# Statistics, routing and turned logits behind the attention step, another front, keys turned by transfers, and eight attention steps per block in a layer of linear attention plus a mixture of experts

## The chip, the cores and the metric

The kernel runs on one core of one Trainium2 chip. The metric is the device time of one execution in microseconds (us), median of the runs shown. The engines are named as in the profile: PE (matrix products and transposes through the array), PEld (its weight loads, beside PE), DVE (vector), ACT (activation), POOL (indirect transfers and accumulating stores, small vector work), SP (issues most of the transfers).

## What is computed

One layer over x of shape (8, 1024, 256), float32. With xn = (x - mean)/sqrt(var + 1e-5) per row:

```python
q, k = elu(xn @ Wq.T) + 1, elu(xn @ Wk.T) + 1;  v = xn @ Wv.T      # 16 heads of 16
out   = q . cumsum(k v) / clip(q . cumsum(k), 1e-6)                # causal linear attention
attn  = out @ Wo.T
logits = x_n @ Wr + br            # 8 experts; the two best, softmax over their two logits
ffn   = sum over the two of  c_e * (silu(xn @ W1[e]) * (xn @ W3[e])) @ W2[e]     # inner width 512
result = x + attn + ffn
```

Here x_n is xn too: both branches take the normalised rows.

## The kernel before, in words

The 8192 rows are 16 **blocks** of 512 rows (t, four chunks c of 128). Two kinds of work share the engines.

**The experts.** Rows are sorted by expert into **tiles** of 128 rows (j); 132 tiles are run here. A tile step (`tile_step`, with `ffn_step` inside) gathers its rows by an indirect transfer on POOL (xg, and a table entry with mean, deviation and weight), normalises them on ACT (L1231), turns them so that features lie on partitions (xgT: tiles below 27 on PE, later ones by a transfer of 16-bit halves, L1241, L1250, L1259), makes gate and up (gu_ps, L1310, 16 products of 128x128x128, 32 records in the profile), silu on ACT (L1318), the product on DVE (hT, L1321), one tile later the product with W2 (y_ps, L1329), its scaling on DVE (y, L1336) and an accumulating scatter on POOL (L1340). W1 and W3 of a tile are loaded by SP two tiles ahead into five buffers.

**The attention.** `attention()` is a generator of steps, block by block (`block_steps`, `project`, `scores`, `carry`, `weigh`, `attend`), and every tile step takes about one of them (`attend_upto`) ahead of its own products. Nine steps make a block: queries (zq L819); keys (zkk L835, then elu on ACT and DVE into kn); the keys turned on PE (tp L882: 8 transposes, kT copied from PSUM by ACT L885) with running sums on DVE (ksum: a scan L887, its last column L891, the product with the queries L892); values (zkv L835, copied into va by ACT L852) and denominators (den L904, then L910 and L911 on DVE and eight transfers of rden by SP); the scores of chunk 0 (s_ps L936, masked by DVE into s_sb L943); and four steps, one for each chunk (o_ps L955, L973, L983, then oT L990 and kv L993 on DVE). PE's order is the program's (`manual_schedule`), DVE's, ACT's and POOL's behind the front is set by a planner from priorities and expected readiness; each engine runs its own list in order.

**The front.** Four blocks are loaded, normalised, turned and routed first (first_moments, normalise, turn, logits, `route`), and `first_batch` makes the list of the first 25 tiles from them: one-hot rows made by ACT (mid_at), POOL (late_at, L650) and DVE (at_first), summed on PE (sum_ps L704), copied by ACT (sums L711), summed again (first_ps L713), made into row numbers (num_i L617). The first gather waits for these. The front is one order written by hand on all engines.

**Tiles 0 to 11** also bring in the other 12 blocks: statistics two blocks at a time (`moments`, L312 to L330), `normalise` (ACT, four a block), `turn` (tp L358, xnT copied by ACT), `logits` (lg_ps L376, copied to lgT by ACT L1424, turned on PE L1437) and, every four blocks, `route` (some fourteen DVE operations L424 to L457, then cnt_ps L463 and L469 on PE). From tile 12 on `second_batch` makes the list of the other tiles in 32 pieces (at_place L591, held L604 and parts L609 on DVE, parts L611 on ACT, held_ps L749 on PE), spread over tiles 13 to 21.

PSUM is eight banks: four of tag mm (gu, z, s_ps), two of tag y (y_ps, lg, den, a_ps, cnt, sum), two of tag t (tp, xg_t, o_ps).

Of the kernel before, what the change touches and what calls it, by code (L numbers as in the profile page):

```python
# [54 lines left out]
P = 128  # L55
# [9 lines left out]
def tile_attention_moe(  # L65
# [38 lines left out]
    WARMING = 14  # L104
# [155 lines left out]
    nc.gpsimd.memset(va, 0.0)  # L260
# [3 lines left out]
    nc.gpsimd.memset(own_of, 0.0)  # L264
# [3 lines left out]
    nc.gpsimd.tensor_scalar(upto_neg, before, -1.0, None, ALU.add)  # L268
    base_row = iota("base_row", E, ROWS, 0, 0)

    for o in range(KC):
        nc.gpsimd.tensor_copy(own_of[:, o, o * HALF : (o + 1) * HALF], own)
# [11 lines left out]
    def first_moments(t):  # L284
# [3 lines left out]
        for c in range(NCH + 1):  # L288
            if c < NCH:
                nc.vector.bn_stats(st[:, c, :], xbs[t][:, c, :])  # L290
            if c > 0:
                nc.vector.bn_aggr(mv[:, c - 1, :], st[:, c - 1, :])
            if t == FB and c == 1:
                yield
# [7 lines left out]
    def moments(t, n):  # L302


# [4 lines left out]
        st = small("st", 6)  # L309
        mv = small("mv", 2)  # L310
        for c in range(n * NCH):
            nc.vector.bn_stats(st[:, c, :], xbs[t + c // NCH][:, c % NCH, :])  # L312
            nc.vector.bn_aggr(mv[:, c, :], st[:, c, :])
# [15 lines left out]
        yield  # L329
        nc.vector.scalar_tensor_tensor(less, mv[:, :, 0], -1.0, rstd, ALU.mult, ALU.mult)  # L330
        yield

    def normalise(t):
        xb = xbs.pop(t)
        less, rstd = (tab[:, t * NCH : (t + 1) * NCH, w] for w in (1, 2))
        for c in range(NCH):
# [5 lines left out]
            else:  # L342
                nc.scalar.activation(
                    xb[:, c, :], xb[:, c, :], AF.Identity, bias=less[:, c : c + 1],
                    scale=rstd[:, c : c + 1],
                )
        scaled[t] = xb
# [56 lines left out]
    nc.gpsimd.memset(new, 1.0)  # L404
    nc.gpsimd.memset(new[:, :, 0:1], 0.0)
# [4 lines left out]
    def route(a, b):  # L410
# [39 lines left out]
        yield  # L450
# [9 lines left out]
        )  # L460
        cnt_ps = ps_y.tile([P, E * n + E], F32, tag="y", name="cnt_ps")
# [9 lines left out]
        )  # L471
        yield
# [14 lines left out]
        den2 = work("den2", n)  # L487
        nc.vector.tensor_scalar(den2, diff, 1.0, None, ALU.add)
        wt = tab[:, tiles, 0]
        nc.vector.reciprocal(wt, den2)  # L490
        second = slice(NT + a * NCH, NT + b * NCH)
        nc.vector.tensor_tensor(tab[:, second, 0], diff, wt, ALU.mult)
        if a > 0:
            nc.vector.tensor_copy(tab[:, second, 1:3], tab[:, tiles, 1:3])
        yield
# [101 lines left out]
    def one_hot(in_row, place, rows, j, a, n):  # L597
# [11 lines left out]
        nc.vector.tensor_scalar(parts[:, :, 0, :], held, row128[:, 0:1], None, ALU.mult)  # L609
# [22 lines left out]
    def first_batch():  # L632
# [7 lines left out]
        late = FT - 2 * PART  # L640
# [3 lines left out]
        less_place = f_one.tile([P, late], F32, name="less_place")  # L644
        nc.scalar.mul(less_place, place[:, 1, 0:late], -1.0)
        place_f = f_one.tile([P, 2 * PART], F32, name="place_f")
        nc.gpsimd.tensor_copy(place_f, place[:, 1, late:FT])
        late_at = [masked.tile([P, PART, P], F32, tag="s_sb", name="late_at") for _ in range(2)]
        for i in range(2 * PART):
            nc.gpsimd.tensor_scalar(  # L650
                late_at[i // PART][:, i % PART, :], cols, place_f[:, i : i + 1],
                number1[:, FT + late + i : FT + late + i + 1], ALU.is_equal, ALU.mult,
            )
        upto = add_up(sizes(False), "upto1")
# [13 lines left out]
        mid_at = [masked.tile([P, PART, P], F32, tag="s_sb", name="mid_at") for _ in range(2)]  # L668
        for i in range(late):
            nc.scalar.activation(  # L670
                mid_at[i // PART][:, i % PART, :], cols, AF.Square,
                bias=less_place[:, i : i + 1],
            )
            nc.scalar.activation(
                mid_at[i // PART][:, i % PART, :], mid_at[i // PART][:, i % PART, :], AF.Relu,
                bias=number1[:, FT + i : FT + i + 1], scale=from_last[:, i : i + 1],
            )

# [9 lines left out]
        yield  # L688
        sum_ps = ps_y.tile([P, P], F32, tag="y", name="sum_ps")
        groups = [(late_at, 2), (None, 0), (mid_at, 0), (mid_at, 1), (None, 1), (late_at, 3)]  # L690
        groups += [(None, 2), (None, 3)]
        for n, (made, g) in enumerate(groups):
            if made is None:
                at = at_places(
                    place, 0, g * PART,
                    e_two.tile([P, PART, P], F32, tag="at_first", name="at_first"),
                )
            else:
                at = made[g % 2]
            if n == 1:  # L700
                yield
            for i in range(PART):
                c = N1 * ((0 if made is None else FT) + g * PART + i)
# [79 lines left out]
    def elu1(dst, z):  # L783

        neg = two.tile([P, TB], F32, tag="neg", name="neg")
# [40 lines left out]
    def mask_q(t, o):  # L826
        qT, qm = blocks[t][0:2]
        for a in range(2):
            nc.scalar.mul(qm[:, o, a, :], qT[:, o, :], par[:, a : a + 1])

    def project_kv(t, c, a):
        z = ps_mm.tile([P, 2, H], F32, tag="mm", name="zkv"[:2] + "kv"[a])
# [8 lines left out]
    def project_k(t, c):  # L841
# [3 lines left out]
            kn[:, c : c + 2, :].rearrange("p c h -> p (c h)"), z.rearrange("p c h -> p (c h)")  # L845
# [11 lines left out]

    def project(t):


        if t > 0:
            begin(t)
            for o in range(KC):
# [3 lines left out]
                yield  # L867
            for c in range(0, NCH, 2):
                for _ in project_k(t, c):
                    pass  # L870
                yield
        else:
            for _ in range(4):
                yield
        qT, qm, kT, kn, va, rden = blocks[t]
        upto_t = two.tile([P, KC], F32, tag="upto_t", name="upto_t")
        fresh = t % BLK_PER_SEQ == 0
        qks = []
        for o in range(KC):
            tp = ps_t.tile([P, TB], F32, tag="t", name="tp")  # L880
            for c in range(NCH):
                nc.tensor.transpose(  # L882
                    tp[:, bass.ts(c, P)], kn[:, c, bass.ts(o, P)], ident
                )
            nc.scalar.copy(kT[:, o, :], tp)  # L885
            ksum = two.tile([P, TB], F32, tag="ksum", name="ksum")
            nc.vector.tensor_tensor_scan(  # L887
                ksum, ones[:, 0:1].to_broadcast([P, TB]), kT[:, o, :],
                0.0 if fresh else sums[0][:, o : o + 1], ALU.mult, ALU.add,
            )  # L890
            nc.vector.tensor_copy(upto_t[:, o : o + 1], ksum[:, TB - 1 : TB])  # L891
            nc.vector.tensor_tensor(ksum, qT[:, o, :], ksum, ALU.mult)  # L892
            qks.append(ksum)
            yield
        for c in range(0, NCH, 2):
            if t > 0:
                for _ in project_v(t, c):
                    pass
            yield

        den = ps_y.tile([P, P], F32, tag="y", name="den")
# [19 lines left out]
        yield  # L921
# [110 lines left out]
    def block_steps(t):  # L1032


        for i, _ in enumerate(project(t)):
            if i in (1, 3, 5, 8):
                yield
# [21 lines left out]
    STEPS = 9  # L1059
    LAST = NBLK * STEPS + 1  # L1060

    TOGETHER = (0, 4, 8)
# [22 lines left out]
    with tc.manual_schedule(engines={EN.DVE, EN.Activation, EN.PE, EN.Pool}):  # L1085
# [9 lines left out]
        next(parts[0])  # L1095
        for t in range(FB):
            next(parts[t + 1])
            next(parts[t])
            normalise(t)
            if t == 2:  # L1100
                nc.scalar.copy(lgT4[:, 0, :], lg_ps.pop(0))
            turn(t)
# [6 lines left out]
            else:  # L1109
                lg_ps[t - 1] = logits(t - 1)  # L1110
        next(parts[FB])
# [425 lines left out]
```

## Time and profile before

| what | us |
|---|---|
| median of 3 runs (lowest, highest) | 1265.2 (1262.7, 1265.59) |
| the profiled execution: its time | 1257.66 |
| its span, first to last instruction | 1255.5 |
| busy: PE, DVE, ACT, POOL | 1205.5, 675.3, 554.5, 527.9 |
| mean granted clock of PE | 0.987 |
| tile 0's gate and up begin | 51.1 |
| tile 2's gate and up begin | 69.1 |
| PE waits over 0.15 us each from 69.1 to 300, sum | 17.4 |

A row of the groups or of the timeline reads: line of the kernel, engine, operation, out<-in, partitions x elements, count; then busy us and mean ns of one; in brackets the engine's idle time ahead of it and what ended that. In the chain of waits each piece follows the one that released it, with start and length in us, and the PE pieces there are start to start, so that they add up to the time that PE's stream needs. Windows give the busy us of each engine in a stretch, and at the end the granted clock, the share of the 16 DMA engines and GB/s.

### The profile page before, as it was taken

Reading aid. Unit: us, or ns where it says so; the run is one execution under the profiler, and the core shown is the slowest. Engines: PE = TensorE matmul, PEld = TensorE weight load, DVE = VectorE, ACT = ScalarE, POOL = GpSimd, SP = SyncE. Lnnn points to the kernel's source line nnn. Section 1 sums busy time; section 2 is a strip of 40 time slices with the busy share of each in tenths; the row PEclk is TensorE's granted clock in tenths of the full one; section 3 lists DMA queues with packets and bytes.
Section 4 is the critical chain, followed back from the end, with each engine's and each line's share of the span. In section 5 each row is a group of like instructions: output and inputs, shape, how many; then the busy total and the mean of one; then the engine's idle time right before and its main releaser. Section 6 shows DMA issues by size and latency. Waiting matters only on the chain.

```text
span 1255.5 us, 29756 instructions
## 1 busy us (share of the span) xinstructions
PE 1205.5 (96%) x11460; PEld 1059.7 (84%) x11460; DVE 675.3 (54%) x1541; ACT 554.5 (44%) x1064; POOL 527.9 (42%) x460
## 2 busy tenths in 40 slices
PE   7788898999999999999999999999999999999994
PEld 5677787888888889888888889989888889898884
DVE  7776669975344544545453545445453545445451
ACT  5665454471624335262625335262626243352610
POOL 4733234325443544444434544444443354444322
PEclk8899999999999999999999999999999999999997
DMA  9788565747987887969888787979897987879672
GB/s 339 274 276 266 150 209 116 237 115 229 245 196 182 193 198 167 244 151 227 177 200 182 187 202 167 223 169 223 185 200 171 189 193 178 205 165 247 145 178 33
DMA packets 203934, 245.84 MB, mean 196 GB/s; under 512 B 72946, under 2 KB 127858, under 8 KB 203506
## 3 DMA queue, kind: packets, MB, share of 16 engines
q1 hardware_dynamic: 161010, 191.79, 52.9%
q0 software_dynamic: 38032, 43.22, 24.6%
q10 hardware_dynamic: 4752, 8.91, 2.0%
q8 instruction: 94, 1.54, 0.5%
q14 instruction: 46, 0.38, 0.1%
HBM read 187.91 MB, written 44.29 MB: 185 GB/s over the span
## 4 chain that ended last, share of the span: by engine, by line
PE 87%; DVE 7%; DMA 2%; ACT 2%; issue 1%; SPq 0%; POOL 0%; POOLq 0%; ACTq 0%; DVEq 0%
PE gu_ps L1310 36%; PE y_ps L1329 17%; PE s_ps L936 5%; PE o_ps L973 5%; PE a_ps L1015 5%; PE zq L819 4%; PE zkk L835 4%; PE zkv L835 4%; PE o_ps L955 2%; DMA xb<-in_x_dram 1%; PE tp L882 1%; PE held_ps L749 1%; PE tp L358 1%; PE den L904 1%; DVE st L312 1%
## 5 line engine op out<-in xcount | busy, mean ns | idle before, releaser
L1310 PE MATMUL gu_ps<-xgT,w 128*128 128x128 f32 x4224 | 504.6, 277 | 6.4 <-issue 2.9
L1310 PEld LDWEIGHTS gu_ps<-xgT,w 128*128 128x128 f32 x4224 | 487.3, 192 | 21.1 <-issue 12.7
L1340 POOL DMA_INDIRECT out_dram<-y,dst_i x107 | 175.4, 1639 | 320.2 <-DVE y L1336 96.8
L1329 PE MATMUL y_ps<-w_sb,hT 128*128 x1056 | 250.9, 380 | 2.1 <-DVE tab L327 1.1
L1218 POOL DMA_INDIRECT xg<-in_x_dram,src_i x132 | 129.0, 977 | 229.1 <-DVE half L1241 114.4
L1329 PEld LDWEIGHTS y_ps<-w_sb,hT 128*128 128x128 f32 x1056 | 190.5, 190 | 24.8 <-issue 1.6
L1318 ACT ACTIVATE hT<-gu_ps 128x512 f32<-128x512 f32 x132 | 78.8, 597 | 286.9 <-PE gu_ps L1310 237.4
L943 DVE TENSOR_TENSOR s_sb<-s_ps,causal 128x512 f32<-128x512 f32 x256 | 159.0, 681 | 70.5 <-PE s_ps L936 68.1
L1321 DVE TENSOR_TENSOR hT<-gu_ps,hT 128x512 f32<-128x512 f32 x132 | 90.3, 684 | 63.0 <-PE gu_ps L1310 28.2
L1223 POOL DMA_INDIRECT entry<-tab_d,of_i x107 | 107.2, 1002 | 39.5 <-issue 31.4
L1336 DVE TENSOR_SCALAR y<-y_ps,entry 128x256 f32<-128x256 f32 x132 | 63.7, 482 | 109.9 <-PE y_ps L1329 109.9
L1241 DVE COPY half<-xg 128x512 uint16<-128x512 uint16 x105 | 47.9, 457 | 130.7 <-ACT xg L1231 130.7
L1020 ACT COPY at<-a_ps 128x256 f32<-128x256 f32 x64 | 23.8, 373 | 173.0 <-PE a_ps L1015 123.0
L1259 ACT COPY xgT<-halfT 128x512 uint16<-128x512 uint16 x105 | 79.7, 759 | 5.1 <-DMA halfT<-half 5.1
L1231 ACT ACTIVATE xg<-xg,entry 128x256 f32<-128x256 f32 x132 | 78.4, 595 | 2.1 <-DMA entry<-tab_d,num_i 2.1
L936 PE MATMUL s_ps<-qm,kT 32*128 32x256 f32 x1024 | 75.3, 400 | 0.1
L1015 PE MATMUL a_ps<-wo_sb,oT 128*128 128x256 f32 x256 | 67.9, 388 | 2.9 <-DVE y L1336 2.0
L973 PE MATMUL o_ps<-s_sb,va 128*32 128x128 f32 x2048 | 69.2, 276 | 0.0
L973 PEld LDWEIGHTS o_ps<-s_sb,va 128*32 128x32 f32 x2048 | 52.0, 109 | 17.8 <-issue 15.9
L1340 POOL DMA_INDIRECT acc_d<-y,src_i x25 | 44.2, 1766 | 52.6 <-DVE y L1336 23.3
L835 PE MATMUL zkv<-wkv_sb,xnT 128*128 128x256 f32 x256 | 59.9, 388 | 0.0
L835 PE MATMUL zkk<-wkv_sb,xnT 128*128 128x256 f32 x256 | 59.4, 386 | 0.0
(228 smaller groups left out, 1339.1 us busy)
## 6 DMA issues: line engine op xcount, KB each, us to landing
w<-in_w_dram SPq DMA_DIRECT2D x264, 512.0 KB
rden<-over SPq DMA_DIRECT2D x128, 64.0 KB
xnT<-xnT_d SPq DMA_DIRECT2D x15, 512.0 KB
out_dram<-at POOLq DMA_DIRECT2D x13, 512.0 KB
out_dram<-in_x_dram SPq DMA_DIRECT2D x12, 512.0 KB
xnT_d<-xnT ACTq DMA_DIRECT2D x11, 512.0 KB
xb<-in_x_dram SPq DMA_DIRECT2D x9, 512.0 KB
w_sb<-in_w_dram SPq DMA_DIRECT2D x4, 1024.0 KB
```

What stands on the lines that cost most here:

```text
L835: nc.tensor.matmul(z[:, i, :], lhsT=xnTs[t][:, k, bass.ts(c + i, P)], rhs=wkv_sb[:, k, a, :], start=(k == 0), stop=(k == KC - 1),)
L936: nc.tensor.matmul(s_ps[r][:, hh].rearrange("p a l -> p (a l)"), lhsT=kT[rows, hh, span], rhs=qm[rows, hh, :, span], start=True, stop=True,)
L943: last_masked[0] = nc.vector.tensor_tensor(sm, s_ps[r].rearrange("p k a l -> p (k a) l"), causal_b, ALU.mult)
L973: nc.tensor.matmul(o_ps[32 * r : 32 * r + 32, hh, :], lhsT=va[:, c, 4 * hh + r, a, :], rhs=s_sb[r][:, 2 * hh + a, :], start=(first and a = ...
L1015: nc.tensor.matmul(a_ps, lhsT=oT[:, hh, :], rhs=wo_sb[:, hh, :], start=(hh == 0), stop=(hh == 1),)
L1218: rows = nc.gpsimd.indirect_dma_start(out=xg[j], out_offset=None, in_=x_rows[:, :], in_offset=bass.IndirectOffsetOnAxis(ap=src_i[:, i : i ...
L1223: nc.gpsimd.indirect_dma_start(out=entry[j], out_offset=None, in_=table[:, :], in_offset=bass.IndirectOffsetOnAxis(ap=num_i[:, i : i + 1], ...
L1259: nc.scalar.copy(xgT[j].bitcast(U16).rearrange("p k (l b) -> p b k l", b=2), halves.pop(j).rearrange("p (b k) l -> p b k l", b=2),)
L1310: done = nc.tensor.matmul(ps[:, i, :], lhsT=w13[:, k, bass.ts(i, P)], rhs=xgT[j][:, k, :], start=(k == 0), stop=(k == KC - 1),)
L1321: nc.vector.tensor_tensor(hT, gu[1], hT, ALU.mult)
L1329: done = nc.tensor.matmul(y_ps, lhsT=hT[:, i, :], rhs=w2_sb[:, bass.ds(e * (IC * H) + i * H, H)], start=(i == 0), stop=(i == IC - 1),)
L1340: nc.gpsimd.indirect_dma_start(out=rows[:, :], out_offset=bass.IndirectOffsetOnAxis(ap=dst_i[:, i : i + 1], axis=0), in_=ys.pop(j), in_off ...
```

## The change

Five edits, all in the one function:

1. **Front.** Constants not needed at once (new, upto_neg, own_of, va) go behind the five square-root calls on POOL; block 0 is normalised ahead of block 1's statistics; one-hot rows: ACT 8 (BY_ACT), POOL 7 (up to BY_POOL = 15; it made 8), DVE 1; queries' and keys' elu and the query masks (mask_q) go behind the list, the masks behind tile 0's turn; 18 idle products at the start instead of 14, four in the routing, 14 of 128 columns ahead of tile 0 instead of 3 of 512.
2. **Statistics, routing, turned logits** of tiles 0 to 11: out of the places ahead of the attention step and behind the tile, to one place directly behind the attention step; statistics one block a tile, the deviations for two.
3. **Lists**: eight tiles of five pieces, 14 to 21; the first factor of `parts` goes from DVE to ACT.
4. **Keys turned by transfers** for blocks 1 to 15: kn is split into 16-bit halves by DVE, four transposing transfers by SP, and ACT joins the halves into kT.
5. **Eight steps**: keys; queries; values, kT and the running sums; denominators, scores of chunk 0; four chunks.

```diff
@@ first_batch
-        late = FT - 2 * PART
...
+        less_place = f_one.tile([P, BY_ACT], F32, name="less_place")
+        nc.scalar.mul(less_place, place[:, 1, 0:BY_ACT], -1.0)
...
+        for i in range(BY_ACT, BY_POOL):
+            at_one(nc.gpsimd, made[i // PART][:, i % PART, :], FT + i, place_p[:, i : i + 1])
@@ one_hot
-        nc.vector.tensor_scalar(parts[:, :, 0, :], held, row128[:, 0:1], None, ALU.mult)
+        nc.scalar.mul(parts[:, :, 0, :], held, row128[:, 0:1])
@@ project
+        key_state[t] = two.tile([P, KC], F32, tag="upto_t", name="upto_t"), []
         if t > 0:
             begin(t)
+            kT, kn = blocks[t][2:4]
+            halves_k = planes("k_half").rearrange("p (c b h) -> p c b h", c=NCH, b=2)
+            for c in range(0, NCH, 2):
+                for _ in project_k(t, c):
+                    pass
+            for c in range(0, NCH, 2):
+                nc.vector.tensor_copy(
+                    halves_k[:, c : c + 2],
+                    kn[:, c : c + 2].bitcast(U16).rearrange("p c (h b) -> p c b h", b=2),
+                )
+            yield
+            turned_k = planes("k_halfT").rearrange("p (b o l) -> p b o l", b=2, o=KC)
+            for c in range(NCH):
+                in_order(
+                    nc.sync.dma_start_transpose(
+                        out=turned_k.rearrange("p b o l -> p (b o) l")[:, :, bass.ts(c, P)],
+                        in_=halves_k[:, c].rearrange("p b h -> p (b h)"),
+                    )
+                )
             for o in range(KC):
                 for _ in project_q(t, o):
                     pass
                 mask_q(t, o)
-                yield
+            yield
             for c in range(0, NCH, 2):
-                for _ in project_k(t, c):
-                    pass
-                yield
...
-        for o in range(KC):
-            tp = ps_t.tile([P, TB], F32, tag="t", name="tp")
-            for c in range(NCH):
-                nc.tensor.transpose(
-                    tp[:, bass.ts(c, P)], kn[:, c, bass.ts(o, P)], ident
-                )
-            nc.scalar.copy(kT[:, o, :], tp)
...
+                for _ in project_v(t, c):
+                    pass
+            for o in range(KC):
+                in_order(
+                    nc.scalar.copy(
+                        kT[:, o].bitcast(U16).rearrange("p (l b) -> p b l", b=2),
+                        turned_k[:, :, o],
+                    )
+                )
+                key_sums(t, o)
             yield
@@ block_steps
-        for i, _ in enumerate(project(t)):
-            if i in (1, 3, 5, 8):
-                yield
+        yield from project(t)
+        denominators(t)
         if t + 1 < NBLK:
             fetch(t + 1)
         waiting = scores(t, 0)
...
-    STEPS = 9
+    STEPS = 8
-    TOGETHER = (0, 4, 8)
+    TOGETHER = (0, 7)
...
@@ the front: what follows the four blocks
-        next(qs[0])
+        keep_busy(4)
         routing = route(0, FB)
...
-        mask_q(0, 0)
...
-        mask_q(0, 1)
...
-        for _ in range(3):
-            idle_ps = ps_mm.tile([P, TB], F32, tag="mm", name="idle_ps")
-            nc.tensor.matmul(
-                idle_ps, lhsT=ident, rhs=blocks[0][0][:, 0, :], start=True, stop=True
-            )
+        keep_busy(14)
...
     ffn_turn(0)
+    for o in range(KC):
+        mask_q(0, o)
@@ tile_step
-    AHEAD = 2 + LISTS // 2 + 3 * (READ - LISTS) // 2
+    AHEAD = 2 + LISTS // 2 + READ - LISTS
...
         def finish():
             if turning:
-                tp = ps_y.tile([P, P], F32, tag="y", name="lg_t")
-                nc.tensor.transpose(tp, held.pop("lgT"), ident)
-                add_logits(t, 1, tp)
-                if (t + 1) % ROUND == 0:
-                    routing = route(t + 1 - ROUND, t + 1)
-                    next(routing)
+                held["lgT"] = f_two.tile([P, P], F32, tag="lgT", name="lgT")
+                nc.scalar.copy(held["lgT"], logits(t))
             if counting:
-                for _ in routing:
-                    pass
-
-        if t + 1 < NBLK:
-            if j % 2:
-                with tc.issue_after((last_token if j < 3 else last_masked)[0].ins):
-                    for _ in moments(t + 1, 2):
-                        pass
-            normalise(t + 1)
+                next(routing)
+            if t + 1 < NBLK:
+                normalise(t + 1)
...
         waits = attend_upto(upto, put_off=True)
+        if t <= NBLK:
+            with tc.issue_after((last_token if j < 3 else last_masked)[0].ins):
+                if "lgT" in held:
+                    tp = ps_y.tile([P, P], F32, tag="y", name="lg_t")
+                    nc.tensor.transpose(tp, held.pop("lgT"), ident)
+                    add_logits(t - 1, 1, tp)
+                if routing and not counting:
+                    for _ in routing:
+                        pass
+                    routing = None
+                if counting:
+                    routing = route(t - ROUND, t)
+                    next(routing)
+                of_blocks = [] if j == 0 else [t + 1, t + 2] if j == 1 else [t + 2]
+                for a in of_blocks:
+                    if a < NBLK:
+                        if a % 2 == FB % 2:
+                            held["mv"] = moments_tile(2)
+                        some = slice(0, NCH) if a % 2 == FB % 2 else slice(NCH, 2 * NCH)
+                        stats(a, held["mv"][:, some])
+                        if a % 2 != FB % 2:
+                            deviations(a - 1, 2, held.pop("mv"))
         piece(1)
```

## The prediction

> **What bounds the kernel now.** I read the busy times first, then the same by stage, then the chain of waits in one block, then the timelines of the front.
>
> ```profile
> PE 1205.5 (96%) x11460; PEld 1059.7 (84%) x11460; DVE 675.3 (54%) x1541; ACT 554.5 (44%) x1064; POOL 527.9 (42%) x460
> ```
> ```profile
> 0.00:69.08 69.08, 53.78 (x398) 41.26 (x398) 48.66 (x191) 39.98 (x85) 37.43 (x63) 0.88 0.89 311
> 69.08:300.00 230.92, 213.14 (x2064) 185.04 (x2064) 171.32 (x509) 120.42 (x315) 83.64 (x65) 0.99 0.67 192
> 300.00:1230.00 930.00, 929.90 (x8953) 825.84 (x8949) 453.21 (x837) 393.08 (x663) 401.14 (x329) 1.00 0.84 193
> 1230.00:1255.50 25.50, 8.68 (x55) 7.57 (x53) 2.14 (x4) 0.97 (x2) 5.70 (x4) 0.74 0.30 36
> ```
>
> The columns are busy us of PE, PEld, DVE, ACT, POOL, then granted clock, DMA share, GB/s. From 300 to 1230 PE is idle 0.1 us of 930: there only PE's own work, or a new wait, moves the time. From 69 to 300 it is idle 17.8 us, in the front 15.3 and at half clock for parts of it. One block in the saturated stage, as the chain of waits has it (start, us), then ACT and DVE beside it:
>
> ```profile
> 618.12 1.73 PE y_ps L1329 x8
> 619.85 0.87 PE tp L882 x8
> ...
> 626.03 3.45 PE zkv L835 x16
> 629.48 0.57 PE den L904 x16
> 630.05 3.77 PE gu_ps L1310 x32
> ```
> ```profile
> 620.32 1.07 ACT L885 COPY kT<-tp 128x512 f32<-128x512 f32 x2 [0.45 <-PE tp L882]
> 629.52 0.65 ACT L852 COPY va<-zkv 128x256 f32<-128x256 f32 x2 [1.08 <-PE zkv L835]
> 632.57 0.76 ACT L1259 COPY xgT<-halfT 128x512 uint16<-128x512 uint16 x1
> ```
> ```profile
> 620.94 2.46 DVE L887 TENSOR_TENSOR_SCAN ksum<-ones,upto_t,kT 128x512 f32<-128x512 f32 x2 [0.22 <-ACT kT L885]
> 623.32 0.27 DVE L891 COPY upto_t<-ksum 128x1 f32<-128x1 f32 x2
> 623.51 1.28 DVE L892 TENSOR_TENSOR ksum<-qT,ksum 128x512 f32<-128x512 f32 x2
> ```
>
> The transposes cost PE 0.87 us a block. Note that the products in ksum are done at 624.8, while den comes at 629.5: the values' step lies between and hides 4.7 us.
>
> **Keys by transfers, eight steps (blocks 2 to 15).** Removed: 0.87 x 14 = 12.2 us of PE. Added on PE: nothing. On DVE two splits of 1024 16-bit elements a block, at least 0.46 (L1241, for 512), at most 0.92; DVE is half idle (453 of 930). On SP four transfers of 1.23 us each, the row of halfT; ahead of them it waits for the splits, behind them stand the next weight load and the next halfT. The weights are due two tiles (some 17 us) later, so I cost this at nothing; if that cover is gone, PE waits for gu. On the DMA engines: in the trace's packet records the 105 transfers of halfT are 53,760 packets of 256 B at 23 ns, 0.74 us of sixteen engines each; 60 more are 45 us, the share goes from 0.84 by 45/1255 to 0.88. Nothing, as long as loads come two tiles early.
>
> [...] A weight packet of 2048 B took 103 ns, so a byte costs 1.8 times as much in a turning packet. [...]
>
> The price is in the new order. In the built program kT is copied on ACT behind the four va copies of the same step, and den opens the next step with nothing between but the tile's own products. With the values' start as zero: second pair of va 3.49 to 4.14 (629.52 - 626.03); kT's first half at 4.04. That copy, 1024 16-bit elements, is not in the trace: at least 1.19 (0.76 + 512 x 0.84 ns, the slope between copies of 256 and 512, 0.373 and 0.588), at most 1.51 (twice 0.76). I take 1.19; a slope is nearer than a doubled fixed part. Then DVE in the built order: scan 1.23, column 0.14, product 0.68, scan 1.23, hT 0.68, column 0.14, half 0.43, product 0.68, less some 0.2 of overlap: 5.0, done at 10.2. PE stands at den at 3.45 + 3.57 + 1.73 = 8.75, does its first half by 9.04 and waits 1.2 us (0.9 to 1.6). Queued behind it on PE: scores, a_ps, the next tile. So a block costs 1.2 - 0.87 = +0.33, 14 blocks **+4.5** (0 to +10). This is the forecast's main point: the transposes go, den is late instead.
>
> **The front.** The first gather waits for this:
>
> ```profile
> 29.62 8.64 POOL L650 TENSOR_SCALAR late_at<-cols,place_f,number 128x128 f32<-128x128 f32 x8
> ```
> ```profile
> 41.69 0.62 PE L713 MATMUL first_ps<-fold,sums 128*128 128x25 f32 x2 [2.53 <-ACT sums L711]
> 57.28 3.21 PE L1310 MATMUL gu_ps<-xgT,w 128*128 128x128 f32 x16 [2.15 <-ACT xgT L1271]
> 86.96 2.02 PE L1310 MATMUL gu_ps<-xgT,w 128*128 128x128 f32 x16 [2.08 <-issue]
> ```
>
> Block 0's normalise comes 3 us earlier, but DVE is full with statistics until block 3's (16.89); only one pair of normalises (0.73) leaves that stretch: routing 0.8 earlier. POOL makes 7 one-hots of 1.08: done 36.5. ACT: 16 operations (6.8 from 28.5) and four of elu (2.45), so sums at 37.8 instead of 41.36, as lgT, va and two masks stood ahead of it. The gather is 3.6 earlier. Behind it 14 idle products take 3.1 us at full clock (0.11 a record) and 5.7 at half (the 14 at the start): tile 0 at 48.7 for 51.1. Tile 1's xgT leaves the queue behind four normalises (2.08): 53 for 57.3. Tile 2 needs the scores' banks, so DVE's list ahead of s_sb (statistics of three blocks, deviations, y, over): 64.4 for 69.1, with 1.08 of scores already done: **-5.8** (-2 to -7).
>
> **Tiles 2 to 12.** PE waits 9.5 us there now, 2.08 of it where scores stand behind routing on DVE (86.96); such waits mostly go. What is late next: lgT is copied between lg and its transpose, 0.45 x 4 where no attention step lies between; and `route`. Its operations start only behind s_sb, oT and kv, with eight channels of statistics in between (4 + 4 x (0.33 + 0.08) x 2, hT, y), so that run is ready some 12 us after the scores, and PE is there after 9.3: 2.8 at tiles 4 and 8. At tile 12 elu and split of the keys do the same: 2.5. Sum 8.1 + 1.8 + 0.6 = 10.5: **+1.0** (-7 to +8).
>
> Idle stretches also cost clock: after waits of 1.93 and 0.75 at 188 to 191 the granted clock was 0.51 from 191.0 to 194.5, worth 1.0 in the eight transposes there (1.91 for 0.87). One such more than now, one less: **+0.5**.
>
> [...]
>
> **Lists, tiles 13 to 21.** DVE is 97% busy from 180 to 240. It loses 32 x 0.33 = 10.5 (L609) and gains 3.4 of splits; PE waits 7.9 there, and ACT, half idle, takes the 32: **-5** (-7.9 to +3). Block 1's 0.87 is given back by its own den.
>
> **Sum.** -5.8 + 1.0 + 0.5 - 5.0 + 4.5 = -4.8, on the profiled 1257.7 (span 1255.5): 1252.9. The median of the runs is 7.5 above that execution; put on the median 1265.2 - 4.8, **1260**.
>
> **Rivals.** *Den not late* (ACT or DVE reach kT sooner, as the planner thought): the 12.2 are kept and nothing is paid, 1265.2 - 9.3 - 12.2 = 1244. For it: DVE and ACT half idle. Against: kT cannot start ahead of va. *Routing hidden too* (DVE's small operations overlap more): waits of tiles 2 to 12 fall to 2, 1260 - 8 = 1252. *Front gains lost* (an entry lands late behind x and W2, DMA share 0.92 to 1.04 from 41 to 58): 1265. *Slower*: den waits for a landing. The transfers stand on SP behind a weight load that waits for a free buffer and a halfT that waits for DVE; if kT's copy starts 1.5 us later than I have it, each block pays 2.7 - 0.87, and the ACT queue behind it (silu, xgT) as well: 14 x 1.8 = 25 for 4.5, less 9.3 of gains, 1265 + 16 = 1281 at worst, some 1272 with half the delay. It decides from a wait of 1.5 us a block on (9.3/14 + 0.87).
>
> **Chances.** Forecast 0.45; den not late 0.15; routing hidden too 0.10; front lost 0.08; slower 0.22. A measurement tells 0.3% (3.8 us) from nothing: faster is both fast rivals and 0.28 of the forecast, 0.53; same 0.17 of it and the lost front, 0.25; slower 0.22. The range goes to 1247 (half of the first rival) and to 1272.
>
> **What would show it.** In the windows of the saturated stage PE idle some 17 us instead of 0.1; PE den waiting 0.9 to 1.6 for DVE ksum, 14 times; PE cnt_ps waiting near 2.8 three times; tile 0 near 48.7, tile 2 near 64.4. Wrong if den does not wait, or if gu waits for weights or xgT.

## The result, and the profile after

| | before | changed |
|---|---|---|
| median of the runs | 1261.5 us (1257.9 to 1267.2, 11 runs) | 1269.4 us (1267.8 to 1271.5, 11 runs) |
| ratio to before | | 1.0059, 95% interval 1.0044 to 1.0074 |
| span of the profiled execution | 1255.5 us | 1268.3 us |

The change made the kernel slower by 0.6%, some 7.4 us by the ratio. I had forecast 4.8 us faster. The profiled execution of before was one of its fastest, so the two traces differ by 12.8 us; sums over the traces below are made against that. Line numbers in the rows are those of the kernel that was run.

The busy times of the changed kernel, and then the windows at the same times as before (columns: window and length; busy us of PE, PEld, DVE, ACT, POOL; granted clock, DMA share, GB/s):

```profile
PE 1197.1 (94%) x11378; PEld 1049.5 (83%) x11378; DVE 687.3 (54%) x1541; ACT 591.7 (47%) x1098; POOL 526.6 (42%) x459
```
```profile
0.00:69.08 69.08, 55.08 (x463) 43.46 (x464) 54.57 (x209) 39.66 (x84) 37.64 (x63) 0.94 0.94 315
69.08:300.00 230.92, 207.55 (x1936) 179.65 (x1934) 155.34 (x457) 141.97 (x347) 79.72 (x64) 0.97 0.68 196
300.00:1230.00 930.00, 912.27 (x8767) 806.70 (x8766) 469.38 (x862) 406.77 (x661) 400.58 (x326) 1.00 0.93 199
1230.00:1268.30 38.30, 22.21 (x220) 19.70 (x218) 8.01 (x15) 3.27 (x7) 8.66 (x7) 0.83 0.31 46
```

PE has 8.4 us less work, and yet the end is later. From 300 to 1230, where PE was idle for 0.1 us, it now is for 17.7. From 69 to 300 its idle time went from 17.8 to 23.4 and the mean clock from 0.99 to 0.97. The groups of PE's instructions say what it waits for (behind the bar: busy us, mean ns; idle us ahead of the group, and what ended it):

```profile
L968 PE MATMUL den<-ksum,own_of 128*32 128x128 f32 x256 | 13.9, 293 | 26.9 <-DVE ksum L897 21.2 <-DVE y L1406 2.9 <-DVE upto_t L896 2.8
L481 PE MATMUL cnt_ps<-both,upto_neg 128*128 128x128 f32 x8 | 1.9, 318 | 6.2 <-DVE den L460 3.7 <-DVE both L456 2.5
L769 PE MATMUL held_ps<-parts,at_place 128*128 128x220 bf16 x128 | 18.4, 262 | 1.9 <-ACT parts L624 1.7 <-DVE at_place L604 0.2
```

den waits 26.9 us, where before it waited for nothing. To see where the two traces part, I take the start of a tile's first gate product (tile 13 as the lists begin, tile 31 when the lists are done and block 3 is at its den), and count for each stretch what PE lost. Work is the number of PE's products times their duration in the saturated stage; half clock (a granted clock of 0.50) and slow starts are busy time above that.

| changed minus before, us | to tile 13 | tile 13 to 31 | tile 31 to the end | sum |
|---|---|---|---|---|
| den's waits | +2.9 | +8.8 | +15.2 | +26.9 |
| other waits of PE | -6.9 | +2.0 | -0.1 | -5.0 |
| work | 0 | -5.3 | -7.8 | -13.1 |
| idle products | +2.0 | 0 | 0 | +2.0 |
| half clock, slow starts | -2.5 | +4.8 | +0.4 | +2.7 |
| time | -4.5 | +10.3 | +7.7 | +13.5 |

(The last product to the end of the span is 0.7 us shorter.) The transposes saved are the 13.1: 15 blocks at 0.87. Of the 5.3 from tile 13 to 31 only 2.6 are transposes; the other 2.7 are a step of attention that the changed kernel does behind tile 31, so at equal work the list stage lost some 13 us and the rest some 5. den's waits are 2.9 in block 0, 3.2 in block 1, 4.3 in block 2 and 16.5 in blocks 3 to 15, 1.27 each.

One block of the saturated stage shows the wait that I had drawn up, ACT, then DVE, then PE:

```profile
643.16 0.65 ACT L879 COPY va<-zkv 128x256 f32<-128x256 f32 x2 [0.78 <-PE zkv L861]
643.70 2.56 ACT L940 COPY kT<-k_halfT 128x1024 uint16<-128x1024 uint16 x2
```
```profile
645.09 1.28 DVE L892 TENSOR_TENSOR_SCAN ksum<-ones,upto_t,kT 128x512 f32<-128x512 f32 x1 [2.78 <-ACT kT L940]
647.20 1.28 DVE L892 TENSOR_TENSOR_SCAN ksum<-ones,upto_t,kT 128x512 f32<-128x512 f32 x1
649.37 0.68 DVE L897 TENSOR_TENSOR ksum<-qT,ksum 128x512 f32<-128x512 f32 x1
```
```profile
646.53 1.89 PE L1399 MATMUL y_ps<-w_sb,hT 128*128 x8
648.35 0.42 PE L968 MATMUL den<-ksum,own_of 128*32 128x128 f32 x8
650.11 0.42 PE L968 MATMUL den<-ksum,own_of 128*32 128x128 f32 x8 [1.33 <-DVE ksum L897]
```

kT's copy begins on ACT the moment the last va copy leaves it, the sums take 5.0 us on DVE behind the first half, and den's second half stands from 648.8 to 650.1. What the keys do not wait for is their transfer: by the trace's packet records the last of the 2,048 packets of 256 B that bring k_halfT begins at 634.4, 9 us ahead of the copy.

In blocks 1 and 2, in the list stage, the same wait is longer: 2.79 and 0.42 ahead of den's two halves in block 1, 2.72 and 1.53 in block 2. ACT and PE, block 1 and then block 2:

```profile
187.42 0.64 ACT L879 COPY va<-zkv 128x256 f32<-128x256 f32 x2
...
191.74 2.55 ACT L940 COPY kT<-k_halfT 128x1024 uint16<-128x1024 uint16 x2
...
196.69 0.43 PE L968 MATMUL den<-ksum,own_of 128*32 128x128 f32 x8 [2.79 <-DVE upto_t L896]
197.53 0.65 PE L968 MATMUL den<-ksum,own_of 128*32 128x128 f32 x8 [0.42 <-DVE ksum L897]
```
```profile
287.18 0.65 ACT L879 COPY va<-zkv 128x256 f32<-128x256 f32 x2 [1.08 <-PE zkv L861]
288.96 0.60 ACT L1388 ACTIVATE hT<-gu_ps 128x512 f32<-128x512 f32 x1 [1.14 <-PE gu_ps L1380]
290.97 0.37 ACT L1341 COPY xgT<-xg_t 128x256 f32<-128x256 f32 x1 [1.41 <-PE xg_t L1337]
...
291.74 2.52 ACT L940 COPY kT<-k_halfT 128x1024 uint16<-128x1024 uint16 x2
...
295.38 0.43 PE L968 MATMUL den<-ksum,own_of 128*32 128x128 f32 x8 [2.72 <-DVE ksum L897]
297.34 0.65 PE L968 MATMUL den<-ksum,own_of 128*32 128x128 f32 x8 [1.53 <-DVE ksum L897]
```

In block 1 kT's copies start 3.7 us behind the last va copy, with the lists' products and a silu between; in block 2 behind a tile's silu and xgT, which wait for PE. (In block 1 DVE adds to it: its first product in ksum stands behind both scans and y.) What these waits do to the clock comes below. One more wait of the list stage is new, at a_ps, for an oT that stands on DVE behind work of the lists:

```profile
225.12 0.61 DVE L617 TENSOR_TENSOR held<-rows,in_row 128x440 bf16<-128x440 f32 x1
225.64 0.42 DVE L1053 TENSOR_TENSOR oT<-rden,o_ps 128x256 f32<-128x256 f32 x1
226.11 1.13 PE L1078 MATMUL a_ps<-wo_sb,oT 128*128 128x256 f32 x4 [3.35 <-DVE oT L1053]
```

It is there, at 1.9 to 3.6 us, in every run below that has the new pieces of the lists, and not in attention_only, which has the old ones; no run tries it alone.

### The profile page after: what moved, and what is told of

It reads as the page before. It is cut to its first block, busy times and chain, and to the rows that moved or that the text cites. A ratio compares the mean times of both kernels' runs of the same rounds, so it can differ in the third digit from the quotient of the medians.

```text
span 1268.3 us, 29751 instructions
## 1 busy us (share of the span) xinstructions
PE 1197.1 (94%) x11378; PEld 1049.5 (83%) x11378; DVE 687.3 (54%) x1541; ACT 591.7 (47%) x1098; POOL 526.6 (42%) x459
## 4 chain that ended last, share of the span: by engine, by line
PE 66%; DVE 4%; issue 2%; ACT 2%; DMA 1%; POOL 0%; POOLq 0%; ACTq 0%; DVEq 0%
PE gu_ps L1380 27%; PE y_ps L1399 13%; PE s_ps L999 5%; PE o_ps L1036 4%; PE a_ps L1078 4%; PE zkv L861 4%; PE zkk L861 4%; PE zq L840 4%; DVE ksum L892 3%; PE o_ps L1018 2%; ACT kT L940 1%; DVE ksum L897 1%; DMA out_dram<-y,dst_i 1%; PE o_ps L1046 0%; PE den L968 0%
## 5 line engine op out<-in xcount | busy, mean ns | idle before, releaser
L1380 PEld LDWEIGHTS gu_ps<-xgT,w 128*128 128x128 f32 x4224 | 491.4, 193 | 17.7 <-issue 10.8
L1286 POOL DMA_INDIRECT xg<-in_x_dram,src_i x132 | 132.0, 1000 | 195.1 <-ACT xgT L1341 71.6
L1078 PEld LDWEIGHTS a_ps<-wo_sb,oT 128*128 128x128 f32 x256 | 47.7, 194 | 19.7 <-DVE oT L1053 5.2
L840 PE MATMUL zq<-xnT,wq_sb 128*128 128x512 f32 x128 | 58.9, 603 | 0.0
```

The costliest lines, as they stand in the source:

```text
L840: nc.tensor.matmul(z, lhsT=wq_sb[:, k, bass.ts(o, P)], rhs=xnTs[t][:, k, :], start=(k == 0), stop=(k == KC - 1),)
L1078: nc.tensor.matmul(a_ps, lhsT=oT[:, hh, :], rhs=wo_sb[:, hh, :], start=(hh == 0), stop=(hh == 1),)
L1286: rows = nc.gpsimd.indirect_dma_start(out=xg[j], out_offset=None, in_=x_rows[:, :], in_offset=bass.IndirectOffsetOnAxis(ap=src_i[:, i : i ...
L1380: done = nc.tensor.matmul(ps[:, i, :], lhsT=w13[:, k, bass.ts(i, P)], rhs=xgT[j][:, k, :], start=(k == 0), stop=(k == KC - 1),)
```

## The experiments

**Theory after the result.** The keys by transfers are cheap in themselves; den is late because kT's copies stand late in ACT's queue (in the saturated stage behind va, in block 1 behind the lists' products, in block 2 behind a tile's silu and xgT), and the long waits of blocks 0 to 2 cost a second time, in clock (6.8 us at 0.50 behind each). Rivals: eight steps are too few, whoever turns the keys; the transfers load the DMA engines; the list stage loses by its own products on ACT. Times are medians; before is 1261 to 1263 in the same hours.

### kt_first: kT ahead of va

```diff
+            for o in range(KC):
+                in_order(nc.scalar.copy(kT[:, o]..., turned_k[:, :, o]))
+                key_sums(t, o)
             for c in range(0, NCH, 2):
                 for _ in project_v(t, c):
                     pass
-            for o in range(KC):
...
```

> The two copies of kT and the sums on DVE behind them are written ahead of the four va copies of the same step; in the built order they move so in blocks 3 to 15, in blocks 1 and 2 nothing moves. Theory (den is late because kT stands behind va on ScalarE; the transposing transfers landed some 9 us before): den's wait of 1.27 us a block and the slower first products behind it (0.21) go in 13 blocks, 13 x 1.48 = 19: 1250. Rival (den waits for the transfers' landing, or the time is lost to DMA load): den waits as before, 1269.

Measured: 1248.3 us, ratio 0.9893 (0.9871 to 0.9914). The same instructions in another order of one queue are worth 21 us. ACT and PE of one block:

```profile
700.35 2.54 ACT L937 COPY kT<-k_halfT 128x1024 uint16<-128x1024 uint16 x2
702.76 1.19 ACT L879 COPY va<-zkv 128x256 f32<-128x256 f32 x4
```
```profile
706.97 0.64 PE L968 MATMUL den<-ksum,own_of 128*32 128x128 f32 x16
```

On DVE the second product in ksum now ends at 705.9; den comes at 706.97 and runs through. A block of the saturated stage takes 68.19 us, for 69.66 in the changed kernel: 1.48 less, which is the wait (1.27) and den's own time (0.58 for 0.79, from its first product to the next group's without the wait, as its products no longer stand in two groups). The landing and the DMA load are out as causes of the wait: the DMA share from 300 to 1230 is still 0.92, and PE is idle there for 2.0 us only. 13 such blocks are 19.2. What else differs between the two traces lies ahead of tile 13: the half-clock stretch from 63.9 to 70.7 in the changed kernel is missing here, though block 0's den waits 2.74 here for 2.90 there. The last section says what may decide that.

### den_late: the first scores ahead of den

```diff
-        denominators(t)
+        if t > 0:
+            waiting = scores(t, 0)
+        denominators(t)
...
```

> The first scores of a block stand ahead of den on TensorE in blocks 1 to 15; ScalarE and the transfers are left as they are. Theory: the scores (1.08) cover most of the wait, 0.3 to 0.4 of 1.27 is left, and as much goes in blocks 1 and 2: 15 x 0.9 = 13.5, 1256. The reciprocal comes some 2.5 us later on DVE, which nothing waits for. Rival (later rden holds up oT): 1269 or more, with waits at a_ps.

Measured: 1263.6 us, ratio 1.0006 (0.9981 to 1.0031): 6 us gained for 13.5 expected. PE in one block:

```profile
712.97 1.89 PE L1404 MATMUL y_ps<-w_sb,hT 128*128 x8
714.79 1.76 PE L999 MATMUL s_ps<-qm,kT 32*128 32x256 f32 x16
716.49 0.65 PE L968 MATMUL den<-ksum,own_of 128*32 128x128 f32 x16
```

den's waits went in the saturated stage, but the scores take 1.76 for 1.15: three of the first four row groups start at 714.79 to 714.81, the fourth at 715.43. On DVE the tile's hT ended at 715.37, behind the second scan; that the fourth bank of the scores is one which hT reads is argued from this order and wasn't tried. A block takes 69.27, 0.4 less than in the changed kernel. If that reading holds, the wait was moved to another product that hangs on the same DVE queue, and the cure has to be ahead of DVE, as in kt_first.

### pe_turn: eight steps without the transfers

```diff
-            halves_k = planes("k_half")...
-            (splits on DVE, four dma_start_transpose)
+            for o in range(KC):
+                tp = ps_t.tile([P, TB], F32, tag="t", name="tp")
+                for c in range(NCH):
+                    nc.tensor.transpose(tp[:, bass.ts(c, P)], kn[:, c, bass.ts(o, P)], ident)
+                nc.scalar.copy(kT[:, o, :], tp)
+                key_sums(t, o)
             for c in range(0, NCH, 2):
                 for _ in project_v(t, c):
```

> The keys are turned on TensorE again (the transfers and the splits on DVE are gone), inside the block of eight steps and with the new front, ahead of the values. Theory: den waits no more (1.48 x 13, and some 5 of the 7.5 us that blocks 1 and 2 wait), the transposes cost 0.87 x 15 = 13: 1269 - 19 - 5 + 13 = 1258. Rival (den's wait is the price of eight steps, whoever turns the keys): 1269 + 13 = 1282. Rival (DMA load slows TensorE's work as well): below 1255.

Measured: 1249.4 us, ratio 0.9895 (0.9873 to 0.9917). So eight steps with the new front beat the kernel before by 1.05% when the keys are turned as of old. The gain over the changed kernel is 20 us for 11 expected. By the trace den's waits fall by 23.7 (3.2 are left, in blocks 0 and 1), other waits by 4.7 (1.4 of it at tile 12's cnt_ps, where DVE had the splits), half clock and slow starts by 3.8; the transposes cost 13.1. What I had missed are the other waits, 2 us of den's and about 1 of clock; the slow starts (13 x 0.21) were in my 1.48 a block. The rival of the DMA load gives such a time too, but not this way: in both kernels a block of the saturated stage has 29.06 us of gate and up products, 13.97 of y and 3.58 of a_ps, each product counted to the start of the next, so PE's work is no slower beside the transfers. A block takes 69.06, so in the saturated stage the changed kernel pays 0.60 a block for having turned its keys without PE.

### attention_only: the kernel before, with the new block of attention alone

```diff
 # in the kernel before: project, key_sums, denominators, block_steps of the changed one, and
-    STEPS = 9
+    STEPS = 8
-    AHEAD = 2 + LISTS // 2 + 3 * (READ - LISTS) // 2
+    AHEAD = 2 + LISTS // 2 + READ - LISTS
```

> The kernel before with the attention block of the changed one alone: keys by transfers, eight steps, den's place, and the step counts of the list stage that go with it; the front, the statistics, the routing, the turned logits and the products of the lists stay as before. Theory (the front and the routing gave 4.5 by tile 13, the lists' products cost 2 to 3, the rest of the loss is in the attention block): 1269 + 4.5 - 2.5 = 1271. Rival (the front's gain is given back later, where TensorE has to wait for something else): 1267 or less; rival (routing moved behind the attention step is what the list stage pays for): 1263.

Measured: 1273.3 us, ratio 1.0086 (1.0056 to 1.0115). The block of attention costs 10.9 us; the front, the statistics, the routing, the logits and the lists' products together give back 3.4 (0.27% between the two ratios, whose intervals overlap, so by the times alone this is not clear). By tile 13 it is 5.6 us behind the changed kernel, by the end 1.8: by the traces the front's gain is real, and two thirds of it are lost from tile 13 on, where the changed kernel's den waits 3.2 in block 1 and this one's doesn't wait. Here kT's copies stand 0.6 us behind the last va copy in that block, and PE has already stood 1.95 at held_ps just ahead of den.

### parts_dve: the lists' products back on DVE

```diff
-        nc.scalar.mul(parts[:, :, 0, :], held, row128[:, 0:1])
+        nc.vector.tensor_scalar(parts[:, :, 0, :], held, row128[:, 0:1], None, ALU.mult)
```

> The 32 products of the lists (L622) go back from ScalarE to DVE; all else as in the changed kernel. Theory (the lists' gain was real, some 4 us at held_ps, but ScalarE's fuller queue costs at den of block 1): the held_ps waits come back (+4), block 1's den wait falls from 3.2 by about 1: 1269 + 3 = 1272. Rival (moving them to ScalarE is the loss in the list stage): 1269 - 5 = 1264 or less.

Measured: 1266.2 us, ratio 1.0024 (1.0009 to 1.0038): some 3 us better than on ACT (the two intervals do not touch), not 3 worse. My theory falls here: the waits at held_ps don't come back (0.8 in its trace, 1.9 in the changed kernel, 5.8 before), so it was not the engine of these products that took them away; attention_only, which has the old times of the lists' pieces, has 6.4 of them. What the products on ACT cost shows in the changed kernel, DVE and then PE:

```profile
236.98 0.62 DVE L617 TENSOR_TENSOR held<-rows,in_row 128x440 bf16<-128x440 f32 x1 [1.02 <-ACT parts L624]
237.51 0.48 DVE L1406 TENSOR_SCALAR y<-y_ps,entry 128x256 f32<-128x256 f32 x1
```
```profile
238.04 1.13 PE L1078 MATMUL a_ps<-wo_sb,oT 128*128 128x256 f32 x4 [0.97 <-DVE y L1406]
```

DVE stands at held until ACT has used up the one before it, y stands behind held, and a_ps needs y's bank. With the products on DVE the two a_ps and one at_ps that wait so take 0.55, 0.94 and 0.41, where there were three waits of 0.97. That is 1.0 us, and held_ps gives 1.1; these two are what the traces show of the 3.

### early_pe: blocks 1 and 2 on TensorE, the rest as kt_first

```diff
+            by_pe = t < 3
 ...
+            if by_pe:
+                (transposes, copy and key_sums as in pe_turn)
+            else:
+                (copies from turned_k and key_sums as in kt_first)
```

> As kt_first (1248.3), but blocks 1 and 2, which stand in the list stage, turn their keys on TensorE, ahead of the values; blocks 3 to 15 use the transfers with kT ahead of va. Theory (what is left of den's wait in kt_first is 3.2 and 4.3 us in these two blocks, because there the built order keeps kT late on ScalarE): as when all blocks turn on TensorE, 1.0 and 0 are left, so 6.5 go, 1.7 come back for the transposes, and some clock: 1243. Rival (the list stage is bound by DVE or by the lists' own work, which fills the place of the wait): 1248.

Measured: 1239.1 us, ratio 0.9826 (0.9796 to 0.9856): 9.2 us below kt_first, 5.3 expected. By the trace 6.8 of den's waits went, 1.2 of other waits, and some 3 of half clock; the transposes cost 1.7. Against pe_turn (1249.4) the transfers in blocks 3 to 15 alone are worth 10.3, close to 13 x 0.87 = 11.3: once kT is copied in time, the transposes do come off nearly whole.

### early_parts: the same, products on DVE

```diff
 # early_pe, and
-        nc.scalar.mul(parts[:, :, 0, :], held, row128[:, 0:1])
+        nc.vector.tensor_scalar(parts[:, :, 0, :], held, row128[:, 0:1], None, ALU.mult)
```

> As early_pe, and the 32 products of the lists (L622) back on DVE. Theory (parts_dve was 3 below the changed kernel, of which 1 was den of block 1, which is gone here): 1 to 2 below early_pe, 1241.5. Rival (the 3 us were all from the waits of ScalarE's queue at den): same as early_pe.

Measured: 1235.9 us, ratio 0.9793 (0.9764 to 0.9823), 3.2 below early_pe; every execution lies below all of early_pe's. The products cost the same 3 us on ACT with and without den's wait in block 1, so it is not through den.

### warm_wait: idle products in den's wait

```diff
         den = ps_y.tile([P, P], F32, tag="y", name="den")
+        for _ in range(12 if t in (1, 2) else 0):
+            nc.tensor.matmul(den, lhsT=ident, rhs=causal, start=True, stop=True)
```

> The changed kernel with 12 idle products into den's own bank ahead of den in blocks 1 and 2 (some 0.22 each at full clock, 2.6 in all); the real products overwrite them. Theory (the waits of 2.8 there cost twice, once as idle time and once by 6.7 us at half clock behind each): den begins as before, the half-clock stretches at 197 and 296 go, 2 x 3.3 = 6.6 come off: 1262.5. Rival (the clock falls for another reason, or the stretch only moves to the next wait): 1269.

Measured: 1263.9 us, ratio 1.0017 (1.0003 to 1.0031), 5.4 us below the changed kernel. In the changed kernel, the waits of blocks 0, 1 and 2 and what follows each (PE busy is the first number behind the length, the clock the third from the end):

```profile
60.30:63.90 3.60, 0.70 (x24) 0.47 (x20) 2.54 (x13) 1.35 (x4) 0.44 (x1) 1.00 1.04 396
63.90:70.60 6.70, 6.36 (x35) 5.30 (x36) 5.90 (x18) 1.66 (x5) 2.18 (x2) 0.50 0.89 268
...
193.90:197.00 3.10, 0.31 (x8) 0.16 (x8) 3.10 (x8) 3.10 (x11) 0.72 (x2) 1.00 0.18 50
197.00:203.80 6.80, 6.38 (x43) 4.44 (x38) 6.51 (x12) 1.77 (x8) 3.00 (x3) 0.50 0.34 46
292.70:296.00 3.30, 0.43 (x8) 0.19 (x8) 3.23 (x5) 1.56 (x2) 2.57 (x2) 1.00 0.27 90
296.00:302.80 6.80, 5.46 (x33) 3.92 (x34) 4.94 (x9) 0.37 (x1) 1.00 (x1) 0.50 0.31 41
```

and in this kernel, blocks 1 and 2:

```profile
195.00:198.50 3.50, 3.50 (x25) 3.26 (x27) 2.07 (x5) 0.35 (x2) 2.62 (x2) 0.51 0.33 37
292.00:296.00 4.00, 2.38 (x32) 1.56 (x28) 3.35 (x7) 0.00 (x0) 1.21 (x2) 1.00 0.32 37
296.00:302.80 6.80, 6.80 (x60) 5.95 (x58) 2.98 (x6) 1.84 (x4) 2.49 (x2) 1.00 0.67 97
```

Each of the three waits is followed by 6.8 us at half clock. With work in the wait, block 2's stretch is gone; in the five traces that have this wait without idle products (kt_first, no_fill, parts_dve, attention_only and the changed kernel) it lasts 6.8. Block 1's is halved, as there den's bank was itself held by y and the idle products waited 2.2 us; but in no_fill and parts_dve it is 3.4 long without them, so for block 1 the effect isn't shown. In block 2, then, the wait of 2.72 cost that and some 3.4 more. By the trace half clock and slow starts fell by 5.8, but 2.0 of this lies ahead of tile 13, where no idle product was added: block 0's stretch is 3.4 here for 6.8.

### no_fill: no idle products ahead of tile 0

```diff
-        keep_busy(14)
```

> The changed kernel without the 14 idle products ahead of tile 0. Theory (an idle TensorE loses its clock): it stands idle for some 5 us ahead of tile 0, the granted clock is near a half for some 3.5 us after that, tile 0's first products take up to 3.5 longer: 1269 + 2 to 3. Rival (tiles 0 and 1 wait for their rows anyway): 1269, with tile 2 where it is now (66.6).

Measured: 1268.5 us, ratio 1.0050 (1.0032 to 1.0067), the same as the changed kernel's 1.0059 within the intervals. The clock does fall (0.50 from 45.9 to 52.7), tile 1 is 1.6 us later. But tile 2 isn't: block 0's den, which waits for DVE, waits 0.87 instead of 2.90, and the half-clock stretch behind that wait goes. The 14 products buy time that the next wait takes back; the rival had it.

### stats_later: block 0's den

```diff
-            with tc.issue_after((last_token if j < 3 else last_masked)[0].ins):
+            with tc.issue_after((last_token if j < 2 else last_masked)[0].ins):
 ...
-                of_blocks = [] if j == 0 else [t + 1, t + 2] if j == 1 else [t + 2]
+                # block FB + 2 in step 1, FB + 3 in step 2, each with its own deviations
```

> As early_parts (1235.9), but the statistics of block 7 move from tile step 1 to 2, and those of tile step 2 are issued behind block 0's reciprocal and masks. Theory (block 0's den, which waits 2.3 to 2.9 for a bank of y, waits for deviations that stand ahead of y on DVE, and this wait costs a half-clock stretch as well): den of block 0 no longer waits, 2.3 + 3.3 go, 1 to 2 come back where the statistics now stand ahead of tile 2 to 4's y: 1232. Rival (DVE is full from 53 to 70, the wait only moves to the next tile): 1236.

Measured: 1233.7 us, ratio 0.9778 (0.9755 to 0.9801), 2.2 below early_parts and 2.2% below the kernel before: the best of all. The step from early_parts is not clear by the times alone, as the intervals and the executions of the two overlap; the trace shows what moved. den of block 0 no longer waits (2.3 gone) and no half-clock stretch follows; 1.4 us come back at the next lg_t, which waits 1.77 for 0.39. The deviations, a chain of short DVE operations from 60.6 to 62.8 in the changed kernel, had stood ahead of the y whose bank den needs.

## Why the prediction was wrong, point by point

- **The front, -5.8.** Tile 0 came at 48.2 (48.7 forecast), tile 1 at 53.1 (53), tile 2 at 66.6 (64.4). The steps up to tile 1 were right. Tile 2's miss is block 0's den: I had the DVE list ahead of the scores, but not that den's bank hangs on y at the end of that list, nor the half clock behind the wait (0.50 from 63.9 to 70.7).
- **Tiles 2 to 12, +1.0 and clock +0.5.** cnt_ps waited 1.66, 2.01 and 1.65 where I had 2.8, 2.8 and 2.5, and lgT's transposes 0.39, 0.89 and 0.38 for 0.45 each. That they cancel is luck: at tile 13 the changed kernel was 4.5 us ahead, and my terms up to there sum to -4.3. The clock, which I had at +0.5, gave -2.5 up to tile 13 and lost 4.8 behind it.
- **Lists, -5.** This is the step that failed, and it failed three times. I let ACT take the 32 products for nothing, as it was half idle; they cost 3 us (parts_dve, early_parts), by holding DVE's held and, behind it, y. And I let block 1's den cost just its 0.87 and block 2's the 1.2 of the saturated stage. They waited 3.2 and 4.3, since in the built order kT's copies stand later there, behind the lists' products in block 1 and behind a tile's silu and xgT in block 2; with the transposes back on PE (early_pe) 1.0 and nothing are left. Each of these waits and block 0's was followed by 6.8 us at half clock. And the other waits of the stage, which I had falling by 5, rose from 7.9 to about 10: held_ps fell from 5.6 to 1.9, but a_ps rose from 1.5 to 6.5, 3.35 of it the one wait for oT. Why that oT stands so late is open, and the best kernel still has it (2.90). From tile 13 to 31 the changed kernel lost 10.3 us where I had it gain 5.
- **The keys, +4.5.** The mechanism and its size were right: den waits 1.27 a block (1.2, 0.9 to 1.6 forecast), for DVE's ksum, behind a kT copy of 1.35 us (1.19 to 1.51) that stands behind va; DVE's chain took 5.0 us as worked out. Mis-sized is only what follows the wait: den's products take 0.79 for 0.58. A block of the saturated stage costs some 0.50 more than before (1.27 + 0.21 - 0.87 - 0.11 of slightly quicker scores and queries) for the 0.33 forecast, 6.5 us in 13 blocks for 4.3.
- **The transfers at nothing.** Right in time, off in load: gu waits for no weights, the DMA share of the saturated stage rose from 0.84 to 0.93, not to 0.88. There are 84,480 packets of 256 B now, at 25 ns for 23. From 300 to 1230 all packets take 80 us more of sixteen engines' time; 48 of that are these, 24 packets of 4 B (52 ns for 30) and 23 packets of 512 and 1024 B, which took 50 ns for 43 and 142 for 132; those of 2048 and 4096 B took 17 less.
- **The rival "slower"** had the better number and the wrong place: it priced a den that waits for a landing. The keys land 9 us early. With 1.6 us a block (24.0 in 15 blocks) den's mean wait did lie above the 1.5 from which I had let it decide.

## What to carry to other kernels

Work that left the bottleneck engine (13.1 us of transposes) came back here as a wait (26.9 us at den), as its replacement sat late in another engine's queue: before pricing the engines, write down for the one consumer (here den) what stands ahead of each of its inputs, in the built order and in every stage apart, not in the saturated stage alone. A half idle engine was not free in a stage where its queue stood between two others: the 32 products on ACT cost 3 us. And price a long wait of PE with what may follow it in clock: behind the waits of 1.65 to 3.53 us told of below that was nothing, or 1.7 us for each 3.4 at half clock, of which one to three followed, by the place where the wait fell; behind those of 1.27 it was nothing.

## What the runs showed of the hardware

The half-clock stretches up to 1200 us (granted clock 0.50) last 3.4 us or a whole multiple of it. In the changed kernel from tile 0 on: 135.6 to 139.0 behind a wait of 2.01; 63.9, 197.0 and 296.0 for 6.8 behind waits of 2.90, 2.79 and 2.72. In parts_dve one lasts 10.2, behind a wait of 3.53 at block 0's den. The drop came 2.6 to 3.6 us after the first four waits began. Length alone does not decide: a wait of 3.35 us in the changed kernel cost no clock,

```profile
222.70:226.10 3.40, 0.06 (x1) 0.00 (x0) 2.87 (x8) 1.79 (x8) 1.58 (x1) 1.00 0.40 152
226.10:233.00 6.90, 6.89 (x102) 6.18 (x103) 4.94 (x11) 2.55 (x8) 1.40 (x2) 1.00 0.17 22
```

a wait of 2.81 at the same product cost a stretch of 3.4 us in pe_turn's run, and one of 1.65 at tile 4's cnt_ps did in early_parts' run and did not in the changed kernel's (1.66). The waits of 1.27 in the saturated stage never did.

The place of the wait on a grid accounts for most of this. The drops of the changed kernel lie 15, 36, 54 and 83 times 3.413 us behind its first one, at 12.69, and within every other trace too they lie whole multiples of 3.413 apart. Along this grid, the stretches ahead of the drops at 63.9 and 135.6, and the two over which the wait of 3.35 is spread:

```profile
60.48:63.89 3.41, 0.66 (x20) 0.46 (x20) 2.35 (x13) 1.25 (x4) 0.43 (x1) 1.00 1.03 396
132.16:135.57 3.41, 1.40 (x21) 0.82 (x20) 3.40 (x20) 2.88 (x8) 1.87 (x2) 1.00 0.58 202
220.90:224.31 3.41, 1.86 (x11) 1.34 (x9) 2.85 (x7) 3.27 (x12) 0.95 (x1) 1.00 0.81 317
224.31:227.72 3.41, 1.61 (x12) 1.31 (x12) 2.51 (x7) 0.55 (x2) 2.89 (x2) 1.00 0.24 33
```

PE was busy for 0.19 and 0.41 of the first two, and for 0.55 and 0.47 of the last two, behind which the clock stayed. Over the twelve traces, from 45 to 1200 us, with each grid laid through the trace's first drop, 3935 such stretches ran at full clock. All 33 in which PE was busy for less than 0.42 were followed by half clock, 8 of the 40 between 0.42 and 0.61, and none of the 3862 above. In kt_first block 0's wait of 2.74 falls into two of them, busy for 0.65 and 0.55, and costs no clock.
